# A decoder layer's cross-attention: weights turned by VectorE blocks and transfers through DRAM, exponentials per head, outputs one step later

## The chip, the cores and the metric

The kernel runs on one core of one Trainium2 chip. The core has engines that run side by side and wait for each other by semaphores: TensorE (PE in the profile, its weight loads PEld), VectorE (DVE), ScalarE (ACT), GpSimd (POOL) and SyncE (SP), whose queue here issues nearly all transfers to 16 DMA engines. SBUF is the working memory of 128 partitions, PSUM the one that TensorE writes to. The metric is device microseconds of one execution, lower is better; all data is float32.

## The reference

One post-norm decoder layer on x of 2 x 1024 x 256, with a context of 2 x 77 x 256, 16 heads of 64. Cut to what matters:

```python
x = _layernorm(x + self_attention(x))              # causal, rotary, Wq Wk Wv Wo, bo
# cross-attention, the part that is changed
q = (x @ w_q)  -> heads;  k, v = (ctx @ w_k), (ctx @ w_v) -> heads   # 77 keys
attn = softmax(q k^T / 8)                          # per head, over the 77 keys
x = _layernorm(x + concat_heads(attn @ v) @ w_o)
# feed-forward for half of the rows of each batch
weights = x @ w_r + b_r
selected = weights > (the 512th largest of 1024)
x = _layernorm(x + where(selected, gelu(x @ W1 + b1) @ W2 + b2, x))
```

## The kernel before

The self-attention runs first (to about 554 us of the profile) and is not touched. Then comes `Prepare`. It folds the cross-attention's weights: `fold_keys` multiplies w_q with the keys of the context into `wqk` (per batch 256 x (16 heads x 77 keys)), so that scores are one product of x1, the output of the first layernorm. `fold_values` multiplies the values with w_o into `vo` (16 x 77 rows of 256 columns per batch). `vo` goes through a DRAM tensor `vo_d` and comes back as `packed[b]`: the 1232 rows in ten chunks of 128 partitions (NK = 10, the last with 80 rows). So the output of a tile is ten products of turned weights with `packed[b]`.

A `Tile_` is 128 tokens; there are 16, eight for each batch. Its methods, with the lines of the profile:

- `scores(hh)` (L946 to L959), for half of the heads: TensorE writes 2 x 308 scores into one of two PSUM buffers `ps_x`; VectorE takes the maxima of eight heads (L953), then adds their negatives to the scores into `e` in SBUF (L955), which frees the PSUM buffer; ScalarE takes the exponentials of 616 columns in one instruction (L959).
- `weights(hh)`: VectorE sums each head (L964) and inverts (L966); GpSimd multiplies (L967).
- `transposes(ahead)`: TensorE turns `e`, ten blocks of 128 x 128 into PSUM (L978), ScalarE copies them into `p_t` (L984, L987). In the same PSUM tile the x1 of the tile three further on is turned (L983, L989).
- `output(midst, when)`: ten products po_cross (L998, two records each); VectorE adds x1 (L1000) and makes the layernorm (L114 to L121, with a power by GpSimd on L120). `close` writes the normalised rows and the router's weight of each row (`weigh`, L785).

The loop over s runs, on TensorE, the scores of tile s+1, the output of tile s-1, the transposes of tile s. In between stand the parts of the `Router` of batch 0 and later batch 1: `spread` (a transpose of the rows' weights and a copy by ScalarE), `reach` (VectorE counts, for the rows of a tile, how many weights they reach, L801), `select`, `slots`, `scatter` (GpSimd writes the rows to DRAM in order, L831), `load` (SP fetches them back). These are set at steps by the tables `ahead`, `at_end` and `midst`. After the loop come the last outputs and the feed-forward of batch 0, the last counts of batch 1, then batch 1's feed-forward.

The order of TensorE, VectorE and ScalarE is written out by hand: each runs its instructions in the order of the program text within the `with tc.manual_schedule(...)` at L1015. In the version before, SP's and GpSimd's order is left to the planner. The weights W1 and W2 of the feed-forward are loaded by two transfers of 1 MB (L95, L101), both issued at 572 us. Pools with `bufs=2` give two buffers to a tag, so the third use waits until the first is no longer read.

Of the kernel before, what the change touches and what calls it, by code (L numbers as in the profile page):

```python
# [20 lines left out]
S = 77  # L21
# [13 lines left out]
def decoder_layer(  # L35
# [55 lines left out]

    def load_wide(w, tag):

        t = wpool.tile([P, NC, INNER], F32, tag=tag, name=f"w_{tag}")
        nc.sync.dma_start(t, w.rearrange("(c p) n -> p c n", p=P))  # L95
        return t

    def load_tall(w):

        t = wpool.tile([P, NP, C], F32, tag="tall", name="w_tall")  # L100
        nc.sync.dma_start(t, w.rearrange("(c p) n -> p c n", p=P))  # L101
        return t
# [572 lines left out]
    class Prepare:  # L675
# [4 lines left out]
        def context(self, of):  # L680

            t = self.pool.tile([P, NP, B, S], F32, name=f"{of}T")
            for h2 in range(0, NP, 2):
# [11 lines left out]
                evacuate(t[:, h2 : h2 + 2, :, :], pk)  # L695
# [34 lines left out]
        def fold_values(self, v_t, b, first=0, last=NP, keep=evacuate):  # L730
# [17 lines left out]
            if last < NP:  # L748
                return
            full = HS // P  # L750
            nc.sync.dma_start(vo_d[b].rearrange("(h s) c -> s h c", s=S), vo)
            nc.sync.dma_start(packed[b][:, :full, :], vo_d[b, : full * P, :].rearrange("(k p) c -> p k c", p=P))
# [170 lines left out]

    class Tile_:


        def __init__(self, b, i):
            self.b, self.i = b, i
            self.x1 = x1s[b][:, i, :C]

        def turn(self):
            self.x_t = c2.tile([P, NC, P], F32, tag="x1T", name="x1T", bufs=3)
            pt = ring.tile([P, NC, P], F32, tag="t", name="pt_x")
            for c in range(NC):
                TE.transpose(pt[:, c, :], self.x1[:, c * P : (c + 1) * P], ident)
            A.copy(self.x_t, pt)

        def scores(self, hh):

            if hh == 0:  # L940
                self.e = c2.tile([P, H, S], F32, tag="e", name="e")
            ps = ps_x.tile([P, 2, NB], F32, tag="sx", name="ps_cross")
            for g in range(2):
# [7 lines left out]
            sc = ps[:, :, : Q * S].rearrange("p g (h s) -> p g h s", h=Q)  # L951
            top = small.tile([P, 2, Q], F32, tag="top2", name="top2")
            V.tensor_reduce(top, sc, AX.X, ALU.max, negate=True)  # L953
            e = self.e[:, hh * HH : (hh + 1) * HH, :]
            V.tensor_tensor(  # L955
                e.rearrange("p (g h) s -> p g h s", g=2), sc,
                top.unsqueeze(3).to_broadcast([P, 2, Q, S]), ALU.add,
            )
            A.activation(e, e, AF.Exp)  # L959

        def weights(self, hh):
            e = self.e[:, hh * HH : (hh + 1) * HH, :]
            sums = small.tile([P, HH], F32, tag="sums2", name="sums2")
            V.tensor_reduce(sums, e, AX.X, ALU.add)  # L964
            inv = small.tile([P, HH], F32, tag="inv2", name="inv2")
            V.reciprocal(inv, sums)  # L966
            G.tensor_tensor(e, e, inv.unsqueeze(2).to_broadcast([P, HH, S]), ALU.mult)  # L967

        def transposes(self, ahead=None):

            self.p_t = c2.tile([P, NK, P], F32, tag="pT2", name="pT2")
            e = self.e.rearrange("p h s -> p (h s)")
            for m in range(0, NK, 4):
                n = min(4, NK - m)
                pt = ring.tile([P, 4, P], F32, tag="t", name="pt_p2")
                for k in range(m, m + n):
                    w = min(P, HS - k * P)
                    self.turned = TE.transpose(pt[:w, k - m, :], e[:, k * P : k * P + w], ident).ins  # L978
                whole = n if (m + n) * P <= HS else n - 1
                if ahead and m + n == NK:  # L980
                    ahead.x_t = c2.tile([P, NC, P], F32, tag="x1T", name="x1T", bufs=3)
                    for c in range(NC):
                        TE.transpose(pt[:, n + c, :], ahead.x1[:, c * P : (c + 1) * P], ident)  # L983
                A.copy(self.p_t[:, m : m + whole, :], pt[:, :whole, :])  # L984
                if whole < n:
                    w = HS - (m + whole) * P
                    A.copy(self.p_t[:w, m + whole, :], pt[:w, whole, :])  # L987
                if ahead and m + n == NK:
                    A.copy(ahead.x_t, pt[:, n : n + NC, :])  # L989

        def output(self, midst=None, when=NK // 2):
# [8 lines left out]
            V.tensor_tensor(y, po, self.x1, ALU.add)  # L1000
            last = layernorm(self.x1, y)

            def close():
                last()
                routers[self.b].weigh(self.i)

            return close
# [7 lines left out]
    with tc.manual_schedule(engines={TE.engine, V.engine, A.engine}):  # L1015
# [3 lines left out]
        tiles[0].turn()  # L1019
        tiles[1].turn()  # L1020
        tiles[2].turn()
        first.fold_keys(k_t)
        v_t = first.context("v")
        first.fold_values(v_t, 0)
        first.fold_values(v_t, 1, 0, NP // 2)
        for hh in range(2):
            tiles[0].scores(hh)
        first.fold_values(v_t, 1, NP // 2, NP, A.copy)
        for hh in range(2):
            tiles[0].weights(hh)  # L1030
        for hh in range(2):
            tiles[1].scores(hh)
        for hh in range(2):
            tiles[1].weights(hh)
# [5 lines left out]
        w1 = load_wide(L0_ffn_W1, "wk")  # L1040
        w2 = load_tall(L0_ffn_W2)
# [19 lines left out]
        for s in range(B * NT - 1):  # L1061
# [13 lines left out]
            elif close:  # L1075
                close()
# [79 lines left out]
```

## Time and profile before

| | |
|---|---|
| time, median of 3 runs | 810.73 us (810.12 to 811.66) |
| profiled execution | 809.84 us |
| its span | 808.1 us |
| PE busy | 781.5 us (97%) |
| PEld, DVE, ACT, POOL busy | 77%, 72%, 44%, 45% |
| granted TensorE clock | 0.998 |
| preparation of the cross-attention | about 554 to 599 us |
| one step of the loop | 9.78 us |
| last output of the cross-attention ends | about 740.4 us |

The span is what the profile covers, from the first instruction to the last; the execution's time has 1.7 us more around it. A row of a timeline has its start, its length, the engine, the line, the operation and what it writes and reads, then how many instructions are merged in it; in brackets stands how long the engine was idle before it and whose work ended that. A row of DMA packets has the queue, the packets, their megabytes, and the time that they took as a share of 16 engines.

### The profile page before, as it was taken

The page shows a single profiled execution, that of the slowest core. Times are in us where ns is not written, and L with a number is a line of the kernel's source. Part 1 is how long each engine was busy: PE and PEld are TensorE (multiplying, and loading weights), DVE is VectorE, ACT ScalarE, POOL GpSimd, SP SyncE. Part 2 cuts the span into 40 slices and gives each one's busy share as a digit, 9 for nine tenths or more (in the row PEclk, how much of TensorE's full clock was granted, in tenths as well). Part 3 has the DMA queues.
Part 4 walks back from the last instruction along what each step waited for, and adds up shares of the span by engine and source line. Part 5 has one row for each costly group of instructions (what it writes and reads, how often), then busy time and mean ns, then how long its engine had stood idle before and what let it go on. Part 6 is the DMA issues. An engine that isn't in the chain of part 4 may idle for free.

```text
span 808.1 us, 26591 instructions
## 1 busy us (share of the span) xinstructions
PE 781.5 (97%) x11428; PEld 622.0 (77%) x11428; DVE 581.9 (72%) x1345; ACT 355.4 (44%) x842; POOL 367.7 (45%) x261
## 2 busy tenths in 40 slices
PE   8999999999999999999999988999999999999986
PEld 5565888888888888788788776688788888886745
DVE  2578678868778868678667796535577788888674
ACT  2565565655565556454554544102433332333130
POOL 2634455555375565365473553222033222261664
PEclk9999999999999999999999999999999999999999
DMA  5455477557567567668366467690450000011221
GB/s 195 129 148 177 129 210 209 171 168 211 157 169 230 158 179 223 174 171 204 112 198 185 133 185 158 173 324 3 168 187 1 1 1 0 1 53 53 68 91 52
DMA packets 65328, 112.32 MB, mean 139 GB/s; under 512 B 6497, under 2 KB 43707, under 8 KB 65211
## 3 DMA queue, kind: packets, MB, share of 16 engines
q1 hardware_dynamic: 59067, 89.64, 37.6%
q10 hardware_dynamic: 4608, 16.78, 7.5%
q0 software_dynamic: 1536, 4.20, 1.4%
q8 instruction: 90, 1.47, 0.8%
q14 instruction: 27, 0.22, 0.1%
HBM read 71.24 MB, written 22.59 MB: 116 GB/s over the span
## 4 chain that ended last, share of the span: by engine, by line
PE 82%; DVE 7%; POOL 4%; issue 4%; ACT 1%; DMA 1%; POOLq 0%; SPq 0%; ACTq 0%; DVEq 0%
PE po_self L410 17%; PE ps_scores L342 16%; PE pp_kq L268 13%; PE pp_v L303 7%; PE po_cross L998 6%; PE ps_cross L946 6%; PE po_proj L477 6%; PE pp_h L889 3%; PE po_ffn L900 2%; PE pt_p L978 1%; DVE pT L372 1%; DMA turned<-raw 1%; POOL comp L831 1%; POOL e L967 1%; DVE p L355 1%
## 5 line engine op out<-in xcount | busy, mean ns | idle before, releaser
L363 ACT ACTIVATE p<-p,neg 128x768 f32<-128x768 f32 (+7 forms) x256 | 196.3, 768 | 162.9 <-DVE neg L355 161.3
L355 DVE CUSTOM_DVE_ANT_0 p<-ps_scores,fence 128x512 f32<-128x512 f32 (+7 forms) x256 | 179.4, 750 | 104.9 <-PE ps_scores L342 104.5
L372 DVE STREAM_TRANSPOSE pT<-p 128x512 f32<-128x512 f32 (+7 forms) x256 | 175.7, 740 | 6.2 <-PE po_self L410 3.0
L410 PE MATMUL po_self<-pT,v 32*64 32x256 f32 (+6 forms) x7808 | 157.6, 295 | 10.1 <-issue 7.2
L410 PEld LDWEIGHTS po_self<-pT,v 32*64 32x64 f32 x7808 | 137.2, 130 | 34.9 <-issue 25.4
L342 PE MATMUL ps_scores<-kq 64*128 64x256 f32 (+3 forms) x1060 | 148.9, 411 | 1.8 <-DVE neg L355 1.0
L342 PEld LDWEIGHTS ps_scores<-kq 64*128 64x128 f32 x1060 | 93.3, 186 | 42.7 <-issue 28.2
L268 PE MATMUL pp_kq<-xT,w_pair 128*128 128x256 f32 (+2 forms) x524 | 118.6, 379 | 1.1 <-ACT xT L203 0.7
L291 POOL TENSOR_TENSOR turned<-turned,sin 128x1024 f32<-128x1024 f32 x31 | 73.2, 2362 | 93.0 <-DMA turned<-raw 80.1
L288 POOL TENSOR_TENSOR kq<-raw,cos 128x1024 f32<-128x1024 f32 x31 | 73.6, 2374 | 84.4 <-ACT raw L276 84.4
L268 PEld LDWEIGHTS pp_kq<-xT,w_pair 128*128 128x128 f32 x524 | 88.3, 190 | 23.9 <-issue 10.4
L967 POOL TENSOR_TENSOR e<-e,inv 128x616 f32<-128x616 f32 x32 | 38.2, 1215 | 113.0 <-DVE inv L966 67.2
L120 POOL TENSOR_TENSOR rs<-ve,neg_half 128x1 f32<-128x1 f32 x48 | 27.2, 570 | 107.2 <-DVE ve L118 105.2
L295 POOL TENSOR_TENSOR kq<-kq,turned 128x1024 f32<-128x1024 f32 x31 | 73.5, 2371 | 1.4
L998 PE MATMUL po_cross<-packed,pT 128*128 128x256 f32 (+1 forms) x320 | 72.5, 380 | 0.1
L946 PE MATMUL ps_cross<-wqk,x1T 128*128 128x308 f32 x256 | 69.2, 423 | 0.0
L998 PEld LDWEIGHTS po_cross<-packed,pT 128*128 128x128 f32 (+1 forms) x320 | 60.0, 190 | 9.4 <-ACT pT L984 0.3
L303 PEld LDWEIGHTS pp_v<-w_pair,xT 128*128 128x128 f32 x512 | 61.1, 192 | 4.0 <-issue 2.5
L303 PE MATMUL pp_v<-w_pair,xT 128*128 128x128 f32 x512 | 62.2, 275 | 0.0
L946 PEld LDWEIGHTS ps_cross<-wqk,x1T 128*128 128x128 f32 x256 | 47.4, 190 | 16.2 <-issue 0.7
L959 ACT ACTIVATE e<-e 128x616 f32<-128x616 f32 x32 | 23.0, 717 | 80.8 <-DVE e L955 80.8
L477 PE MATMUL po_proj<-wo,attnT 128*128 128x256 f32 x224 | 51.4, 381 | 0.3 <-ACT out_pair L424 0.3
(128 smaller groups left out, 817.0 us busy)
## 6 DMA issues: line engine op xcount, KB each, us to landing
turned<-raw SPq DMA_DIRECT2D x64, 256.0 KB, 4.7
v<-v_d ACTq DMA_DIRECT2D x32, 512.0 KB, 6.2
v<-v_d SPq DMA_DIRECT2D x32, 512.0 KB, 11.1
v_d<-v SPq DMA_DIRECT2D x16, 512.0 KB, 4.6
over<-inv_d SPq DMA_DIRECT2D x32, 256.0 KB, 4.8
attn_d<-out_pair SPq DMA_DIRECT2D x14, 512.0 KB, 4.3
attnT<-attn_d SPq DMA_DIRECT2D x8, 512.0 KB, 5.4
vo_d<-vo SPq DMA_DIRECT2D x2, 1232.0 KB
```

The source lines that it names most:

```text
L268: TE.matmul(pp[:, cols], self.w[:, c, "kq".index(of), :], x_ts[self.b, n][:, c, cols], start=(c == 0), stop=(c == NC - 1),)
L288: E.tensor_tensor(self.kq[:, :, n * NB : (n + 1) * NB], self.raw[n], self.twice(cos, n), ALU.mult)
L295: E.tensor_tensor(dst, dst, self.turned[n], ALU.add)
L303: TE.matmul(pv[:, i, :], x_ts[self.b, 2 * n // NT][:, c, toks], self.w[:, c, 2, :], start=(c == 0), stop=(c == NC - 1),)
L342: TE.matmul(self.ps[j][:, cols], self.kq[rows, 1, t * P : (t + 1) * P], self.kq[rows, 0, cols.start - at : cols.stop - at], start=True, st ...
L355: V.tensor_tensor_reduce(p[:, span], self.ps[j][:, span], fence[:, T - (t + 1) * P :], -SCALE, -MASKED, ALU.add, ALU.min, neg[:, i : i + 1],)
L363: A.activation(p[:, span], p[:, span], AF.Exp, bias=neg[:, i : i + 1], scale=-1.0, accum_out=self.sums[:, j, t : t + 1],)
L372: V.transpose(p_t[:, first : first + t * step + 1 : step, :], self.p[g, j][:, span].rearrange("p (n k) -> p n k", k=P),)
L410: ins = TE.matmul(self.po[r][j * D : (j + 1) * D, n:, :], self.v4[rows, NT * k + n, j * D : (j + 1) * D], p_t[rows, first:last:step, k * R ...
L477: TE.matmul(self.po, of, wo[:, c, :], start=(c == 0), stop=(c == NP - 1))
L946: TE.matmul(ps[:, g, : Q * S], self.x_t[:, c, :], wqk[:, c, self.b, h : h + Q, :].rearrange("p h s -> p (h s)"), start=(c == 0), stop=(c = ...
L998: TE.matmul(po, self.p_t[:w, k, :], packed[self.b][:w, k, :], start=(k == 0), stop=(k == NK - 1))
```

## The change

Five things are changed, all in the cross-attention.

1. The exponentials. VectorE only takes the maxima (`most`). ScalarE takes the exponentials of each head apart, straight from PSUM, with the negative maximum as bias and the sum of the head as second output (`exponentials`): 16 instructions for a tile. The addition and the sum on VectorE go away. The inversion and the multiplication become a function that is called later (`weights`).
2. The turning of weights for tiles 0 to 14. `blocks` lets VectorE turn 32 x 32 blocks of the whole `e` (1280 columns, the last 48 zero) into `part`, reading every fourth column, so that a row of `part` holds for each of four column classes 320 numbers. `part` goes to DRAM in one transfer; `fetch` brings it back in four, one for 32 tokens each, into the layout of `p_t`: runs of 32 numbers, 128 bytes. Tile 15 is still turned by TensorE.
3. The output of a tile comes two steps after its scores' step instead of one (`tiles[s - 2].output()` beside `tiles[s + 1].scores`). `e` gets two fixed buffers, `e_all`.
4. SP's order is now part of the order written by hand. The two halves of `packed[0]` follow the first fetch; those of `packed[1]` stand at the ends of steps 3 and 4; W1 and W2 are loaded in four transfers of 512 KB at the ends of steps 5 to 8.
5. The preparation is ordered anew: scores of tiles 0 to 3 stand between the products of `Prepare`, and their copies are mostly given to VectorE (`keep=V.tensor_copy`). The x1 transposes of tiles 3 and 4 are there too; later ones follow the output in each step. The router's parts move by a step or within a step.

```diff
+        def pack(self, b, h):
             full = HS // P
-            nc.sync.dma_start(vo_d[b].rearrange("(h s) c -> s h c", s=S), vo)
-            nc.sync.dma_start(packed[b][:, :full, :], vo_d[b, : full * P, :].rearrange("(k p) c -> p k c", p=P))
+            a, e = (0, full // 2) if h == 0 else (full // 2, full)
+            nc.sync.dma_start(packed[b][:, a:e, :], vo_d[b, a * P : e * P, :].rearrange("(k p) c -> p k c", p=P))
+            if h == 0:
+                return
             nc.sync.dma_start(packed[b][: HS - full * P, full, :], vo_d[b, full * P :, :])
...
+    e_all = c1.tile([P, 2, NK * P], F32, name="e_all")
+    G.memset(e_all[:, :, HS:], 0.0)
...
-            sc = ps[:, :, : Q * S].rearrange("p g (h s) -> p g h s", h=Q)
-            top = small.tile([P, 2, Q], F32, tag="top2", name="top2")
-            V.tensor_reduce(top, sc, AX.X, ALU.max, negate=True)
-            e = self.e[:, hh * HH : (hh + 1) * HH, :]
-            V.tensor_tensor(
-                e.rearrange("p (g h) s -> p g h s", g=2), sc,
-                top.unsqueeze(3).to_broadcast([P, 2, Q, S]), ALU.add,
-            )
-            A.activation(e, e, AF.Exp)
-
-        def weights(self, hh):
-            e = self.e[:, hh * HH : (hh + 1) * HH, :]
-            sums = small.tile([P, HH], F32, tag="sums2", name="sums2")
-            V.tensor_reduce(sums, e, AX.X, ALU.add)
-            inv = small.tile([P, HH], F32, tag="inv2", name="inv2")
-            V.reciprocal(inv, sums)
-            G.tensor_tensor(e, e, inv.unsqueeze(2).to_broadcast([P, HH, S]), ALU.mult)
+        def most(self, hh):
+            self.top = small.tile([P, 2, Q], F32, tag="top2", name="top2")
+            V.tensor_reduce(self.top, self.split(hh), AX.X, ALU.max, negate=True)
+
+        def exponentials(self, hh):
+
+            sums = self.sums = small.tile([P, HH], F32, tag="sums2", name="sums2")
+            sc, top = self.split(hh), self.top
+            for h in range(HH):
+                g, q = divmod(h, Q)
+                A.activation(
+                    self.e[:, hh * HH + h, :], sc[:, g, q, :], AF.Exp, bias=top[:, g, q : q + 1],
+                    accum_out=sums[:, h : h + 1],
+                )
+            inv = small.tile([P, HH], F32, tag="inv2", name="inv2")
+
+            def weights():
+                V.reciprocal(inv, sums)
+                e = self.e[:, hh * HH : (hh + 1) * HH, :]
+                self.ready = G.tensor_tensor(e, e, inv.unsqueeze(2).to_broadcast([P, HH, S]), ALU.mult).ins
+
+            return weights
+
+        def blocks(self):
+
+            part = c2.tile([P, 4, NK * R32], F32, tag="part", name="part")
+            V.transpose(
+                part.rearrange("p c (k q) -> p c k q", q=R32), self.whole.rearrange("p (k q c) -> p c k q", q=R32, c=4)
+            )
+            part_d = dram.tile([P, 4, NK * R32], F32, tag="part", name="part_d")
+            nc.sync.dma_start(part_d, part)
+            self.p_t = c2.tile([P, NK, P], F32, tag="pT2", name="pT2")
+
+            def fetch():
+                for g in range(4):
+                    rows = slice(g * R32, (g + 1) * R32)
+                    nc.sync.dma_start(
+                        self.p_t[:, :, rows], part_d[rows, :, :].rearrange("j c (k q) -> (j c) k q", q=R32)
+                    )
+
+            return fetch
...
-    with tc.manual_schedule(engines={TE.engine, V.engine, A.engine}):
+    with tc.manual_schedule(engines={TE.engine, V.engine, A.engine, nc.sync.engine}):
...
+        tiles[0].scores(0)
+        tiles[0].scores(1)
+        held = most(tiles[0])
+        v_t = first.context("v", V.tensor_copy)
+        for f in held:
+            f()
+        first.fold_values(v_t, 0, 0, NP // 2)
+        fetch = tiles[0].blocks()
+        first.fold_values(v_t, 0, NP // 2, NP)
+        fetch()
+        first.pack(0, 0)
+        first.pack(0, 1)
+        tiles[1].scores(0)
+        tiles[1].scores(1)
+        held = most(tiles[1])
+        first.fold_values(v_t, 1, 0, NP // 2, V.tensor_copy)
+        for f in held:
+            f()
+        tiles[2].scores(0)
+        kept = [t.turn() for t in tiles[3:5]]
+        tiles[2].scores(1)
+        tiles[2].most(0)
+        tiles[1].blocks()()
+        for keep in kept:
+            keep(V.tensor_copy)
+        held = [tiles[2].exponentials(0)]
+        tiles[2].most(1)
+        held.append(tiles[2].exponentials(1))
+        first.fold_values(v_t, 1, NP // 2, NP - 2, V.tensor_copy)
+        tiles[3].scores(0)
+        first.fold_values(v_t, 1, NP - 2, NP, V.tensor_copy)
+        tiles[3].scores(1)
+        for f in held:
+            f()
...
-        for s in range(B * NT - 1):
-            if s > 0:
-                for hh in range(2):
-                    tiles[s + 1].scores(hh)
...
-            close = tiles[s - 1].output(midst.get(s), NK - 2) if s > 0 else None
-            tiles[s].transposes(tiles[s + 3] if s + 3 < B * NT else None)
...
+        bulk = {
+            5: lambda: nc.sync.dma_start(w1[:, 0, :], wide1[:, 0, :]), 6: lambda: nc.sync.dma_start(w1[:, 1, :], wide1[:, 1, :]),
+            7: lambda: nc.sync.dma_start(w2[:, :m, :], tall2[:, :m, :]), 8: lambda: nc.sync.dma_start(w2[:, m:, :], tall2[:, m:, :]),
+        }
+        for s in range(2, B * NT - 1):
+            t = tiles[s + 1]
+            for hh in range(2 if s > 2 else 0):
+                t.scores(hh)
+            t.most(0)
+            held = [t.exponentials(0)]
+            ahead.get(s, none)()
+            tiles[s].blocks()()
+            t.most(1)
+            held.append(t.exponentials(1))
+            counts.get(s, none)()
+            held[0]()
+            norm = tiles[s - 2].output()
+            if s + 3 < B * NT:
+                tiles[s + 3].turn()()
+            close = norm()
+            held[1]()
+            close()
+            at_end.get(s, none)()
+            if s in (3, 4):
+                first.pack(1, s - 3)
+            elif s in bulk:
+                bulk[s]()
+        close = tiles[-3].output()()
         tiles[-1].transposes()
+        close()
+        norm = tiles[-2].output(lambda: (r1.spread(4, 6), reaches(r1, range(4), 4, 6)), 4)
```

## The prediction

> **What bounds the kernel now.** I read the chain of waits first, cut to the cross-attention stage, then busy times in the same steps, then the DMA packets. The chain, in order of time (start, length, what):
>
> ```profile
> 609.00 4.15 PE ps_cross L946 x16
> 613.15 4.32 PE po_cross L998 x20
> 617.47 1.09 PE pt_p L978 x10
> 618.56 0.22 PE pt_p L983 x2
> 618.78 4.15 PE ps_cross L946 x16
> ```
>
> One step of the loop is 9.78 us, and TensorE fills all of it: scores 4.15, outputs 4.32, ten transposes of weights 1.09, two of x1 0.22. Nothing else ever ends last. The busy times of that step (length, PE, PEld, DVE, ACT, POOL, clock, DMA share, GB/s) show what is left over elsewhere:
>
> ```profile
> 608.84:618.62 9.78, 9.78 (x51) 8.10 (x50) 7.06 (x15) 3.09 (x8) 2.93 (x3) 1.00 0.01 2
> ```
>
> VectorE has 2.7 us free, ScalarE 6.7, and the DMA engines do nothing at all. So a microsecond off TensorE is a microsecond off the time here, until something else takes 8.7 us per step.
>
> **TensorE's part.** The ten transposes leave TensorE for tiles 0 to 14; tile 15 keeps them. 15 x 1.09 = 16.4 us gained, the whole of the gain. Scores, outputs and x1 transposes stay, so the new step is 4.15 + 4.32 + 0.22 = 8.69 us.
>
> **ScalarE.** Two exponentials of 616 (0.72 each) and five copies of transposes (1.24 + 0.28) become 16 exponentials of 77 with a bias and a sum. The nearest rows are the self-attention's, which have both:
>
> ```profile
> 322.51 0.39 ACT L363 ACTIVATE p<-p,neg 128x128 f32<-128x128 f32 x1
> 322.80 0.19 ACT L363 ACTIVATION_READ_ACCUMULATOR p<-p,neg 128x1 f32 x1
> 322.90 0.70 ACT L363 ACTIVATE p<-p,neg 128x512 f32<-128x512 f32 x1
> ```
>
> From one start to the next after it, 128 elements take 0.39 us, reading the sum included. The same line takes 493 ns at 256 elements and 388 at 128, 0.82 ns an element, so 77 elements take 0.39 - 0.04 = 0.35. Per step 16 x 0.35 + one copy of x1 0.39 = 6.0 us. If nothing overlapped it would be 0.35 + 0.19 = 0.54 each and 9.0 us, above 8.69. I take 6.0, since the row shows the overlap directly.
>
> **VectorE.** Gone: two additions (0.80 each) and two sums (0.76 each), 3.1 us. Added: one block transpose of 1280 columns. Its row in the self-attention takes 1199 ns for 1024 and 1059 for 896, so 1280 take 1199 + 256 x 1.09 = 1.48; its input now steps over four elements, which no row shows: 1.48 if that costs nothing, 3.0 if it halves the rate. I take 1.5, as the row. VectorE falls from 7.06 to about 5.5 us per step; the counts of the router add 2 to 3.2 in six steps, 8.7 at worst, level with TensorE.
>
> The score buffers (two in PSUM) are freed later, after eight exponentials instead of one addition. Following one step from its start: scores(0) done at 2.1, maximum until 3.1, exponentials until 5.9; the block transpose holds the second maximum until 5.4, its exponentials end at 8.7. The buffers are wanted at 8.7 and 10.8. Covered, by 2 us.
>
> **The DMA path, the new resource.** Each tile now sends 640 KB to DRAM (rows of 5 KB) and fetches 640 KB in four transfers of runs of 128 bytes: 5120 packets, 320 for each of 16 DMA engines. SP's queue is in program order, so a fetch waits for its store to land, and the next store stands behind that fetch. No row shows packets of 128 bytes. Three windows bound them (packets in 0.5 us at 4 bytes, the load of b1; in 1 us at 1 KB; in 0.8 us at 512 bytes):
>
> ```profile
> q1 hardware_dynamic: 712, 0.02, 88.7%
> ...
> q1 hardware_dynamic: 377, 0.39, 109.3%
> ...
> q1 hardware_dynamic: 521, 0.27, 112.7%
> ```
>
> Engine time over packets: 0.5 x 16 x 0.887 / 712 = 10.0 ns at 4 bytes; 46 ns at 1 KB; 28 ns at 512 bytes. The three lie on one line, so 128 bytes take about 14 ns, with 10 and 28 as the ends. A fetch is 320 x 14 = 4.5 us (3.2 to 9.0). A store at the 426 GB/s of the window 574.5 to 576.0 is 1.5 us. Between a store's last bytes and the first of the load that waits for it stands this (start, length on SP):
>
> ```profile
> 597.31 0.39 SPq L752 DMA_DIRECT2D packed<-vo_d  x1
> ```
>
> The store's last packets end near 596.9 and this load's first come near 598.3, 1.4 us. The fastest landing of a 512 KB store is 3.3 us against 1.3 for its bytes; I take 1.8. So one tile occupies the path for 1.5 + 1.8 + 4.5 = 7.8 us, less than 8.69, with 0.9 to spare. Hiding the latency: blocks end 5 us into a step and the outputs of that tile start 4.2 us into the step after next, 16.6 us later; the path needs 1.1 + 7.8 + 0.5 = 9.4. That is what the step of delay covers.
>
> The spare is used up where other transfers share the queue: two halves of packed_1 (1.6 us each, steps 3 and 4) and four loads of 512 KB for W1 and W2 (1.3 us, steps 5 to 8), which before ran at 572 to 603 beside nothing. There the path takes 9.1 to 9.4 us, 0.4 to 0.7 above TensorE's step, and the stall falls on po_cross.
>
> **Start and end.** Before, preparation kept TensorE full (44.1 of the 45 us from 554 to 599). Now scores wait for exponentials: following the order by hand with the prices above, scores of tile 2 and 3 wait 0.1, 0.6, 0.8 and 0.8 us for their buffers, since VectorE also empties all of vo_1 (eight copies of 0.69): 2.3 us. The fetch for tile 2 comes behind the store of vo (1.2 MB, 4.5 us at 267 GB/s): 0.2. Steps 5 to 9 then wait 0.7, 0.4, 0.5, 0.5, 0.5 = 2.6. At the end tile 14 is needed only 14 us after its step began, while scattered rows share the engines: 1.0. From the last output on (740.4) nothing differs.
>
> Sum: -16.4 + 2.3 + 0.2 + 2.6 + 1.0 = -10.3 us. The profiled execution took 809.84 (span 808.1 and 1.7 around it): 799.5. The median is 0.9 above it: 800.4.
>
> [...] The row shows 4-byte packets of 10 ns and no step below 512 bytes. [...]
>
> **Rivals.**
> Packets (slower). Beyond 8.69 us the path sets the step, 13 times. The gain left after start and end is 13 us; 6 us of other transfers come on top, so it turns to a loss where 13 x (cycle - 8.69) + 6 > 13: a cycle of 9.2, a fetch of 5.9, a packet of 18.5 ns. At the 512-byte row's pitch (0.8 x 16 / 521 = 24.6 ns): fetch 7.9, cycle 11.2, 13 x 2.5 + 6 - 13 = +26 us, 836. For: no such packet in the trace, and a wide window of strided 512-byte reads shows 56 ns (336 packets in 1 us at 118.5%). Against: the 10 ns row.
> Fully hidden (faster still). At 10 ns the cycle is 6.5 and with other transfers 8.1: only start and end cost, -16.4 + 3.3, so 797.6. For: the 4-byte row. Against: 512 bytes cost 28.
> An engine's chain binds. If the stepped transpose takes 3.0 us, the second exponentials end 1.5 later and VectorE needs up to 10.2 in the six counting steps: about 1 us each, 806.5. If exponentials don't overlap, 0.3 x 13: 804. For: neither form is in the trace. Against: its nearest rows.
> No change, 810: packets near 18 ns.
>
> **How the numbers follow.** Forecast 0.42, fully hidden 0.13, engine chain 0.11, packets 0.30, no change 0.04. Predicted 800.4; its own range is 797 to 805. Eight times in ten: 795, below fully hidden, to 826, which leaves out half of the packet rival (0.15). About 0.2% is what a measurement tells from no change: faster 0.64, same 0.04, slower 0.32.
>
> **What would show it.** Right: steps of 8.7 us from the tenth tile on with po_cross back to back; fetches of 4.5 us; 0.35 us between exponentials; a transpose of 1.5. Wrong: po_cross idle behind the fetched tile in every step (packets), ps_cross idle behind an exponential (chain), or SP's issue of a fetch taking more than the 0.64 us that b1's load took.

## The result, and the profile after

The changed kernel takes 818.51 us (median of 4 runs, 816.33 to 819.46) beside 810.67 for the kernel before (4 runs): a ratio of 1.0092, 95% interval 1.0069 to 1.0114. It is 0.9% slower, where 1.3% faster was forecast. The span of the profiled execution is 816.5 us, 8.4 above that of before.

TensorE lost its transposes, as meant. Its busy time fell from 781.5 to 773.9 us, and yet its share of the chain that ended last fell from 82% to 72%, with DMA's up from 1% to 6%. These are the page's totals and the chain's shares by engine:

```profile
PE 773.9 (95%) x11278; PEld 609.7 (75%) x11278; DVE 581.7 (71%) x1306; ACT 388.8 (48%) x1251; POOL 368.0 (45%) x262
...
PE 72%; DVE 9%; DMA 6%; POOL 5%; issue 4%; ACT 2%; SPq 1%; POOLq 0%; DVEq 0%; ACTq 0%
```

So TensorE does less and waits more. The busy times of four stretches from one output to the next (columns as in the forecast's table: stretch, length, PE, PEld, DVE, ACT, POOL, clock, DMA share, GB/s) show three kinds of step:

```profile
703.87:712.64 8.77, 8.77 (x40) 7.10 (x40) 7.95 (x18) 5.38 (x33) 3.38 (x4) 1.00 0.66 149
662.76:673.20 10.44, 9.64 (x42) 7.21 (x40) 9.64 (x23) 5.64 (x34) 2.90 (x3) 1.00 0.82 179
641.41:652.31 10.90, 8.85 (x41) 6.83 (x39) 10.04 (x19) 6.90 (x41) 2.90 (x3) 1.00 0.79 173
652.31:663.43 11.12, 10.86 (x41) 8.42 (x41) 6.81 (x15) 4.67 (x28) 2.94 (x3) 0.85 0.70 165
```

The first is the step that was forecast, with TensorE full for 8.77 us. In the second VectorE is busy for 9.64 of 10.44. The third ends with a wait for a fetch. The fourth has the whole of TensorE's time taken, but at a clock of 0.85.

TensorE's own instructions in order of time (start, length; in brackets the idle time ahead and who ended it) show the third and fourth:

```profile
645.95 4.31 PE L943 MATMUL ps_cross<-wqk,x1T 128*128 128x308 f32 x16
652.31 6.27 PE L1011 MATMUL po_cross<-packed,pT 128*128 128x256 f32 x20 [2.05 <-DMA pT<-part_d]
```

Before, 20 records of po_cross took 4.48 us. Here they wait 2.05 for p_t, and then take 6.27.

What the fetch was late for is seen in SP's queue. First a stretch with a load of W1, then one without:

```profile
645.88 3.42 SPq L988 DMA_DIRECT2D pT<-part_d  x4
649.34 0.79 SPq L1114 DMA_DIRECT2D w<-in_L_ffn_W_dram  x1
650.22 0.38 SPq L982 DMA_DIRECT2D part_d<-part  x1
657.22 3.80 SPq L988 DMA_DIRECT2D pT<-part_d  x4
...
688.86 3.55 SPq L988 DMA_DIRECT2D pT<-part_d  x4
692.52 0.85 SPq L982 DMA_DIRECT2D part_d<-part  x1
696.29 3.49 SPq L988 DMA_DIRECT2D pT<-part_d  x4
```

From fetch to fetch the path takes 7.43 us without other loads (7.8 was forecast), and 11.34 with one (9.1 to 9.4 was). From store to fetch it is 3.77 against 7.00: the load in front of the store costs 3.2 us, not its own 1.3. This is the largest case: behind the other three loads of W1 and W2 store to fetch is 5.7 to 6.0 us and the cycle 10.5 to 10.6, and the two further cycles without a load are 7.8 and 7.4. VectorE isn't in this: the blocks that the store at 650.22 takes, tile 6's, were done at 643.76.

From 658 to 700 us, where the path needs 10.5 us for each tile, VectorE does too, and there the chain that ended last does not touch TensorE at all. One turn of it (start, length, what), from one maximum (`top`) to the next; `part` is the block transpose, `reach` the router's counting, `e_all` GpSimd's multiply, `rs` its power for the layernorm, `x` the layernorm's last instruction:

```profile
662.40 0.71 DVE top L954
663.11 2.40 DVE part L978
665.52 0.68 DVE top L954
666.20 2.77 DVE reach L794 x10
...
669.26 1.15 POOL e_all L971
670.43 0.56 POOL rs L108
671.01 1.31 DVE x L109
...
672.84 0.71 DVE top L954
```

A turn is 10.44 us. Two pieces are longer than the rows that the forecast went by: the block transpose at 2.4 to 2.5 us, and the layernorm's last instruction, 1.31 us, where L121 took 0.41 before for the same 256 columns:

```profile
609.68 0.41 DVE L121 TENSOR_SCALAR x<-y,mv,rs 128x256 f32<-128x256 f32 x1 [0.66 <-POOL rs L120]
```

One piece of the forecast is seen as it was meant. ScalarE's exponentials follow each other at 0.31 us, the read of the sum included:

```profile
663.21 0.33 ACT L962 ACTIVATE e_all<-ps_cross,top 128x77 f32<-128x77 f32 x1 [4.00 <-DVE top L954]
663.43 0.19 ACT L962 ACTIVATION_READ_ACCUMULATOR e_all<-ps_cross,top 128x1 f32 x1
663.52 0.32 ACT L962 ACTIVATE e_all<-ps_cross,top 128x77 f32<-128x77 f32 x1
```

And so is the price of a packet: 4 us in which little but a fetch ran (697 to 701) hold

```profile
q1 hardware_dynamic: 4230, 0.54, 85.0%
```

that is 4 x 16 x 0.85 / 4230 = 12.9 ns for each packet (14 was forecast).

**A measure for what follows.** The same program up to the changed stage reaches the product for the keys (pp_k) between 548.5 and 560.5 us in the fourteen traces of this case, and what follows the last po_cross takes 67.4 to 70.1. So beside the ratio to the kernel before, which ran on the same chip each time, I give the *stage*: from the start of pp_k to the end of the last po_cross in the profiled execution. It is 186.1 us before and 190.8 after; the forecast meant 175.8. Each stage is of one execution. Four kernels (the changed one and those of experiments 3, 9 and 11) are the same up to the fetch of tile 2. Its output waits 2.44, 3.72, 4.14 and 1.83 us for that fetch in their traces, and then takes 4.56 to 6.89, so two stages with the path through DRAM can differ by 4.6 us without a reason in the change.

### The profile page after: what moved, and what is told of

Its sections match the earlier page's. It is cut to its first block, busy times and chain, and to the rows that moved or that the text cites. A ratio compares the mean times of both kernels' runs of the same rounds, so it can differ in the third digit from the quotient of the medians.

```text
span 816.5 us, 26772 instructions
## 1 busy us (share of the span) xinstructions
PE 773.9 (95%) x11278; PEld 609.7 (75%) x11278; DVE 581.7 (71%) x1306; ACT 388.8 (48%) x1251; POOL 368.0 (45%) x262
## 4 chain that ended last, share of the span: by engine, by line
PE 72%; DVE 9%; DMA 6%; POOL 5%; issue 4%; ACT 2%; SPq 1%; POOLq 0%; DVEq 0%; ACTq 0%
PE po_self L398 17%; PE ps_scores L330 16%; PE pp_kq L256 12%; PE pp_v L291 6%; PE po_proj L465 6%; PE po_cross L1011 4%; PE pp_h L882 3%; PE ps_cross L943 2%; DMA turned<-raw 2%; DVE part L978 2%; DVE reach L794 2%; PE po_ffn L893 2%; DMA part_d<-part 2%; DMA pT<-part_d 2%; POOL e_all L971 1%
## 5 line engine op out<-in xcount | busy, mean ns | idle before, releaser
L962 ACT ACTIVATE e_all<-ps_cross,top 128x77 f32<-128x77 f32 x256 | 79.0, 337 | 61.0 <-DVE top L954 59.8
L256 PEld LDWEIGHTS pp_kq<-xT,w_pair 128*128 128x128 f32 x524 | 88.9, 192 | 23.8 <-issue 10.6
L1011 PE MATMUL po_cross<-packed,pT 128*128 128x256 f32 (+1 forms) x320 | 76.1, 394 | 12.0 <-DMA pT<-part_d 9.9
L971 POOL TENSOR_TENSOR e_all<-e_all,inv 128x616 f32<-128x616 f32 x32 | 38.9, 1220 | 105.4 <-DVE inv L969 105.0
L1011 PEld LDWEIGHTS po_cross<-packed,pT 128*128 128x128 f32 (+1 forms) x320 | 62.1, 197 | 23.5 <-issue 8.0
L962 ACT ACTIVATION_READ_ACCUMULATOR e_all<-ps_cross,top 128x1 f32 x256 | 56.1, 219 | 0.0
```

Of the source, the lines that this page charges most:

```text
L256: TE.matmul(pp[:, cols], self.w[:, c, "kq".index(of), :], x_ts[self.b, n][:, c, cols], start=(c == 0), stop=(c == NC - 1),)
L962: A.activation(self.e[:, hh * HH + h, :], sc[:, g, q, :], AF.Exp, bias=top[:, g, q : q + 1], accum_out=sums[:, h : h + 1],)
L1011: TE.matmul(po, self.p_t[:w, k, :], packed[self.b][:w, k, :], start=(k == 0), stop=(k == NK - 1))
```

## The experiments

T1 is the theory that the transfer path sets the loss, T2 that VectorE's chain does. All diffs are against the changed kernel.

**1. Longer runs.**

```diff
-    self.p_t[:, :, rows], part_d[rows, :, :].rearrange("j c (k q) -> (j c) k q", q=R32)
+    self.p_t.rearrange("p k n -> p (k n)")[:, g * NK * R32 : (g + 1) * NK * R32],
+    part_d[rows, :, :].rearrange("j c n -> (j c) n")
```

> The fetch brings the same bytes in runs of 1280 B (512 packets a tile) instead of 128 B (5120); they land in another order within a row of p_t, so the weights of a block of four tiles of tokens are mixed up and the output differs. Theory T1 (the transfer path of one queue, its small packets above all, sets the loss): landing of a fetch falls from 6.1 us after its first issue to under 4, the path cycle without extras from 7.6 to under 6, both waits of 2.44 and 2.05 us for pT go, and with them the two po_cross of 6.2 us; time 803 to 808. Theory T2 (VectorE's chain in the counting steps sets it): the steps around 663 to 694 us keep 10.4 us, only the first waits go; time 811 to 814.

Measured: 801.40 us, ratio 0.9878 (0.9799 to 0.9958); stage 179.0. No po_cross waits for pT, and a tile's twenty take 4.48 to 4.57 us throughout. A fetch is issued in 1.74 us instead of 3.42. But pt_r, the transpose of `spread`, still waits 1.09 and 1.53 us for `route`, the rows' weights by VectorE. T1 holds for the larger part: 11.8 us of the stage hang on the fetch.

**2. The block transpose's stride.**

```diff
-    part.rearrange("p c (k q) -> p c k q", q=R32), self.whole.rearrange("p (k q c) -> p c k q", q=R32, c=4)
+    part.rearrange("p c n -> p (c n)"), self.whole
```

> The block transpose reads e in plain order (stride 1) instead of every fourth column; size and output the same, so the rows of p_t no longer belong to the rows of packed and the output differs. T2: the transpose takes 1.5 us instead of 2.48, VectorE is busy 8.7 instead of 9.7 us in steps 7 to 9, their period falls to 9.5, time 813 to 816. T1: the transpose gets shorter, but the fetch issues in steps 5 to 8 stay 10.5 us apart; 817.5 to 819. If the stride is not the reason, the transpose stays at 2.48 us.

Measured: 813.55 us, ratio 1.0068 (1.0030 to 1.0105); stage 189.8. The group of the transpose (busy, mean ns, idle before) in the changed kernel and in this one:

```profile
L978 DVE STREAM_TRANSPOSE part<-e_all 128x1280 f32<-128x1280 f32 x15 | 37.2, 2483 | 3.2 <-POOL e_all L971 3.2
```
```profile
L978 DVE STREAM_TRANSPOSE part<-e_all 128x1280 f32<-128x1280 f32 x15 | 22.5, 1502 | 3.6 <-POOL e_all L971 3.6
```

The stride costs 0.98 us for each tile, 15 us of VectorE's time in all. Taking it away moves the stage by 1.0, which is less than one wait differs between traces; the interval of the ratio overlaps that of the changed kernel, and 1.0068 of 810.67 us, 816.2, lies between the two expectations. The fetches bind: po_cross waits 2.96, 3.94, 1.17, 0.57, 1.07 and 2.31 us for them. Why every fourth column takes 2483 ns and plain order 1502 is not shown; no run tried another stride.

**3. Loads on another queue.**

```diff
-    5: lambda: nc.sync.dma_start(w1[:, 0, :], wide1[:, 0, :]),
+    5: lambda: nc.scalar.dma_start(w1[:, 0, :], wide1[:, 0, :]),
...
```

> The four loads of W1 and W2 in steps 5 to 8 are issued on ScalarE's queue instead of SP's; nothing else moves. T1 in its form 'one queue': store to fetch in those steps falls from 5.7 to 7.0 us towards 3.8, the fetch issues come 8.7 to 9 us apart instead of 10.5, time 811 to 814. T1 in its form 'shared DMA engines': the bytes still share the engines, store to fetch stays above 5 us, time 816 to 818. T2: steps 7 to 9 keep 10.4 us, since VectorE is busy 9.7 of them, at most 1.5 us come back; 817 to 818.5.

Measured: 813.36 us, ratio 1.0025 (0.9984 to 1.0066), so about 0.7% better than the changed kernel. Its profile is of one of its longer executions (817.5 us), with a stage of 193.6 us, so the two readings don't agree. From 662 to 730 us no output waits for a fetch, but steps of 10.1 and 10.6 us remain, now with pt_r waiting 1.04 and 1.44 us for `route`. Store to fetch is 3.3 to 4.8 us behind those four steps, as the form 'one queue' has it. Before that stand waits of 3.72 us (tile 2, behind the store of vo), 1.39 and 3.51 (behind the halves of packed_1, still on SP's queue), and at the end one of 3.25. It is inconclusive on how much time the four loads cost; it does show VectorE's chain next in line.

**4. No transfers at all.**

```diff
-    part_d = dram.tile([P, 4, NK * R32], F32, tag="part", name="part_d")
-    nc.sync.dma_start(part_d, part)
-    self.p_t = c2.tile([P, NK, P], F32, tag="pT2", name="pT2")
...
+    self.p_t = packed[self.b][:, :, :P]
+    return lambda: None
```

> The store of the blocks and the four fetches of each tile are left out, the block transpose stays; the outputs of tiles 0 to 14 use a part of packed in place of the weights, so the output differs. T1: no wait for pT, no po_cross over 4.6 us, W loads no longer matter; all steps but those held by spread at 8.7 us; time 798 to 803. T2: the first waits go, but steps 7 to 9 keep 10.0 to 10.5 us; time 806 to 811.

Measured: 798.52 us, ratio 0.9858 (0.9790 to 0.9926); stage 179.0, the same as with long runs. It fits neither theory alone. The time is T1's, but from 651.8 us on the steps take 10.1, 10.6, 8.7 and 11.0: in the first two pt_r waits 1.09 and 1.54 us for `route`, in the last the scores wait 0.64 and 0.75 for exponentials, and T1 allowed more than 8.7 only where `spread` holds a step. By the ratios the changed kernel lies 19 us above this one (13 to 25 by the two intervals), more than the 11.8 of the stages; where the rest lies stays open.

**5. Straight into p_t.** The blocks lie in SBUF, and p_t does too; the way through DRAM isn't needed.

```diff
-    part_d = dram.tile([P, 4, NK * R32], F32, tag="part", name="part_d")
-    nc.sync.dma_start(part_d, part)
...
-    self.p_t[:, :, rows], part_d[rows, :, :].rearrange("j c (k q) -> (j c) k q", q=R32)
+    self.p_t[:, :, rows], part[rows, :, :].rearrange("j c (k q) -> j c k q", q=R32)
```

> The store of the blocks to DRAM is left out: four transfers a tile go from the blocks in SBUF straight into p_t, with the same 5120 runs of 128 B; the output is the reference's. Theory T1 (the transfer path sets the loss) in the form 'store, wait and fetch in a row': the transfers start where the blocks end instead of 2.3 to 3.7 us later, nothing is queued behind a wait for a store, all waits for pT over 0.5 us go; from the start of pp_k to the last po_cross 179 to 182 us (before 186.1, after 190.8, without transfers 179.0), time 0.986 to 0.992 of before. T1 in the form 'the small packets': 5120 packets keep their 6.1 us to landing, waits for pT remain in the steps with loads of W1 and W2; 184 to 188 us, 0.995 to 1.003 of before.

Measured: 807.28 us beside 812.97, ratio 0.9921 (0.9893 to 0.9949); stage 179.8. One wait for pT is left, 1.64 us at the last fetched tile. So 5120 packets of 128 bytes for each tile do fit, if no store and no wait between stands in their row: the first form of T1. Here they come from SBUF and not from DRAM, so the small packets of the old fetch aren't tried alone; with long runs (experiment 1) the store and the wait stayed and were hidden as well. What is left binds in VectorE, seen in three steps of this run (columns as above):

```profile
651.50:661.60 10.10, 9.03 (x41) 6.98 (x39) 9.30 (x23) 5.65 (x34) 2.90 (x3) 1.00 0.62 129
661.60:672.20 10.60, 9.17 (x40) 7.07 (x40) 9.80 (x27) 5.55 (x34) 2.91 (x3) 1.00 0.60 116
681.00:691.80 10.80, 9.54 (x43) 7.27 (x41) 9.88 (x19) 5.39 (x33) 4.03 (x4) 1.00 0.49 81
```

VectorE is busy for all of them but 0.8 to 0.9 us, the most of which is L109's wait for GpSimd's power (0.66).

**6. L109 first.** On top of the direct transfer:

```diff
-                def close():
+                def close(between=lambda: None):
                     last()
+                    between()
                     routers[self.b].weigh(self.i)
...
-            close = norm()
-            held[1]()
-            close()
+            norm()(held[1])
```

> As the direct transfer, and in each step the last instruction of the layernorm (L109) is put ahead of the second reciprocal and GpSimd's second multiply instead of behind them. Theory T2 (the rest of the loss is VectorE's chain, in which L109 is held by GpSimd's multiply): L109 falls from a mean of 1.04 or 1.30 us to 0.41 in the steps, the waits of pt_r for route (1.09 and 1.53 us without transfers) fall by 0.9 each or more, 1 to 3 us less than the direct transfer alone. If L109 is not held by GpSimd: it keeps its length, and the second multiply, now later, delays the next blocks; 0 to 2 us more.

Measured: 808.12 us, ratio 0.9914 (0.9875 to 0.9953); stage 179.7, no less. L109's mean over its 32 instances with x fell from 740 to 528 ns, and pt_r's waits from 1.07 and 1.43 to none and 0.87. All of it was given back: GpSimd's second multiply now comes later, and the idle time of the block transpose behind it grew from 3.2 to 7.8 us over the fifteen. L109 does hang on GpSimd's multiply, and moving it alone brings nothing.

**7. TensorE turns again.** Part of the change undone: `tiles[s].transposes()` stands where `blocks` and the fetch stood.

> TensorE transposes all tiles as in the kernel before (ten transposes a tile, ScalarE copies them), the block transpose and its transfers are gone; the exponentials by ScalarE, the outputs one step later and the loads in pieces stay. T1 and T2 alike: no wait for pT, the step is 9.78 us again. If the other two parts of the change cost and gain nothing but the 2.3 us at the start and 1 at the end: 0.999 to 1.006 of before. If they carry part of the loss (ScalarE's sixteen exponentials with three copies more, the order of VectorE): 1.008 or more. If the later outputs bring something by themselves: under 0.998.

Measured: 855.15 us, ratio 1.0500 (1.0450 to 1.0549). That is over the 1.008 of the second outcome, but far over, and for a reason that none of the three names. The steps take 11.7 us. ScalarE's copies into p_t wait 3.8 us in the mean (48.8 over 13 waits) for po_cross of two tiles before, whose buffer they fill: transposes two steps ahead of the output need three buffers, and ScalarE's exponentials, and TensorE behind them, stand behind the copy. So it said nothing on the other parts, and was run again with the third buffer.

```diff
-    self.p_t = c2.tile([P, NK, P], F32, tag="pT2", name="pT2")
+    self.p_t = c2.tile([P, NK, P], F32, tag="pT2", name="pT2", bufs=3)
```

> TensorE transposes all tiles, as in the earlier run of this form, but with three buffers of p_t, so that ScalarE's copies no longer wait for the output of two tiles before. If that wait was the reason for its step of 11.7 us: the step falls to 9.8 to 10.2 us, stage 190 to 198 us, time 1.005 to 1.02 of before. If it was ScalarE's order (copies between two groups of exponentials, which TensorE's scores wait for): the step stays above 11 us, 1.03 to 1.05.

Measured: 824.83 us, ratio 1.0220 (1.0175 to 1.0265); stage 203.3, over the 198 expected. Where nothing is counted, outputs come 9.79, 9.78 and 9.78 us apart: the step of before, to 0.01 us. So exponentials by ScalarE and outputs one step later neither cost nor gain there, and the step's gain is all in the transposes. In the counting steps `spread`'s copy now waits behind ScalarE's copies and exponentials, 1.8 to 2.1 us each time; that cost belongs to this form alone, and how the two other parts do at the ends stays open.

**8. The stride again, with the transfers hidden.** Direct transfer and plain order of e together.

> As the direct transfer, and the block transpose reads e in plain order (so the rows of p_t no longer belong to the rows of packed; the output differs). T2 (with the transfers hidden, VectorE's chain is the limit in the counting steps, 9.3 to 9.9 us busy of 10.1 to 10.8): each of these steps gives back about 1.0 us, the stage from pp_k to the last po_cross falls from 179.8 to 175 to 177 us. If the remaining wait is not VectorE's work but the chain through GpSimd's multiplies and ScalarE: 179 to 180 as with L109 put first.

Measured: 799.56 us, ratio 0.9878 (0.9834 to 0.9923); stage 177.8, 2.0 less than the direct transfer alone. That is less than T2's 2.8 to 4.8. Its parts are larger: up to the output at 630.38 us it is 1.9 shorter, from there to the one at 704.21 another 2.8, and the second wait of pt_r falls from 1.43 to 0.43. The end gives 2.7 back, since the last fetch is waited for 2.18 us (1.64 there), and the eight and twelve records of po_cross behind it take 3.04 and 3.20 us (1.97 and 2.76 there).

**9. Loads behind the store.** The same bytes on the same queue, in another order:

```diff
     nc.sync.dma_start(part_d, part)
+    behind()
...
-    if s in (3, 4):
-        first.pack(1, s - 3)
-    elif s in bulk:
-        bulk[s]()
+    more = (lambda: first.pack(1, s - 4)) if s in (4, 5) else bulk.get(s - 1, none)
+    tiles[s].blocks(more)()
```

> The changed kernel with its halves of packed_1 and of W1 and W2 issued right behind the store of the blocks (steps 4 to 9) instead of ahead of it; every byte stays on SP's queue. T1 (the path is a sum on one queue: what stands ahead of a store delays it, and the fetch behind it, by the whole of its transfer): the extra runs in the store's own latency of 2 us and more; store to fetch falls from 5.7 to 7.0 us to 4 to 5, stage from 190.8 to 184 to 188 us, time 1.000 to 1.006 of before. If the bytes alone count (the engines are full): the fetch now waits behind the extra instead, same sum, 189 to 192 us.

Measured: 809.64 us, ratio 1.0015 (0.9990 to 1.0041); stage 189.9. The ratio is as T1 had it, the stage is not. In SP's queue the order did what was meant:

```profile
651.16 0.33 SPq L982 DMA_DIRECT2D part_d<-part  x1
651.53 0.43 SPq L1115 DMA_DIRECT2D w<-in_L_ffn_W_dram  x1
654.60 3.56 SPq L989 DMA_DIRECT2D pT<-part_d  x4
```

Store to fetch is 3.4 us with 512 KB between them, where the load in front made it 7.00. In the other three steps with loads of W1 and W2 it is 3.5 to 3.8, and 2.9 to 3.1 in the next four without. So most of what the load cost was its place, and about 0.5 us its bytes. From 630 to 720 us no output waits for a fetch; the counting steps still take 10.1 and 10.6 us, through pt_r's waits of 1.07 and 1.43. The rest of this profile's stage is at the start, where the fetch of tile 2 came 4.14 us late behind the store of vo and the po_cross behind it took 6.89 us. In the changed kernel these were 2.44 and 6.24; the difference of 2.35 us is not the order's, so the order gained more than the stage shows.

**10. VectorE's order, with the transfers hidden.** On top of the direct transfer, the last counting instruction of steps 6 to 10 moves between GpSimd's second multiply and L109, so that both waits of the chain are filled with work. In step 9 the moved one also counts 128 columns that had an instruction of their own, some 0.3 us less work:

```diff
+    after_held = {
+        6: lambda: r0.reach(2, 0, 4), 7: lambda: r0.reach(3, 0, 4), 8: lambda: r0.reach(4, 0, 6),
+        9: lambda: r0.reach(5, 0, 7), 10: lambda: r0.reach(6, 0, NT),
+    }
...
     held[1]()
+    after_held.get(s, none)()
     close()
```

> As the direct transfer, and in steps 6 to 10 the last counting instruction (0.74 to 1.27 us) stands between GpSimd's second multiply and L109; the output is the reference's. T2 with the lock between GpSimd and VectorE: the multiply runs beside the counting, L109 falls from 1.3 to 0.41 us there and its wait of 0.66 us for rs goes; 1.3 to 1.5 us less in each of steps 6 to 10, so stage 179.8 to 174 to 177 us, time 0.982 to 0.988 of before. If counting is held by the multiply as L109 was: it gets longer by about the same 0.9 us, 178 to 180 us.

Measured: 798.29 us beside 808.21, ratio 0.9873 (0.9834 to 0.9912); stage 176.1, 3.7 less than the direct transfer alone (the intervals of the two ratios overlap a little, and the traces show where the 3.7 come from). VectorE in one of these steps (start, length):

```profile
665.75 0.19 DVE L969 RECIPROCAL inv<-sums 128x8 f32<-128x8 f32 x1
665.87 1.09 DVE L794 TENSOR_SCALAR_CACHE_REDUCE reach<-every,route 128x896 f32<-128x896 f32 x1
666.88 0.08 DVE L794 DVE_READ_ACCUMULATOR reach<-every,route 128x1 f32 x1
666.88 1.02 DVE L109 TENSOR_SCALAR x<-y,mv,rs 128x256 f32<-128x256 f32 x1
```

and GpSimd beside it:

```profile
666.54 1.22 POOL L971 TENSOR_TENSOR e_all<-e_all,inv 128x616 f32<-128x616 f32 x1
```

The wait for `rs` is gone. GpSimd's multiply runs from 666.54 to 667.76; counting beside it takes 1.09 us for 896 columns (1.14 in the kernel before), and L109, which begins inside it, ends at 667.90, again just behind its end: 1.02 us, where 0.41 was expected. The lock of the expectation is a name for no more than this: L109 ends just behind the multiply that it begins in, and counting beside the multiply keeps its length. What makes the two differ is not shown. This version is faster than both kernels.

**11. Both orders, through DRAM.** The loads behind the store and the late counting, with store and fetches as they are in the changed kernel:

> The changed kernel with its store to DRAM and fetches as they are, and both orders mended: the halves of packed_1 and of W1 and W2 go right behind the store of the blocks, and the last counting instruction of steps 6 to 10 stands between GpSimd's second multiply and L109. The output is the reference's. Theory of two limits of about the same height (the path and VectorE's chain, each of which takes over when only the other is relieved: 189.8 us for the stage with the one, 189.8 with a shorter block transpose): together they bring 4 to 7 us more than the loads behind the store alone, stage 183 to 186 us, time 0.992 to 0.998 of before; what stays are the waits for pT at the start (tile 2, 2 to 4 us) and at the end (2 to 4 us), and po_cross at half clock behind them. If the path alone is the limit and the store must go to gain anything: 188 to 190 us, 1.000 to 1.006 of before.

Measured: 807.01 us beside 809.46, ratio 0.9961 (0.9933 to 0.9990); stage 180.3, below the 183 expected. One order alone left the stage at 189.9 (loads), and a VectorE lighter by 1 us in each step at 189.7; both orders give 9.5 us more than the loads alone. That part includes the start, where tile 2 waited 1.83 us here and 4.14 there, with 2.3 us more in its output behind it: 4.6 of the 9.5, which the edit has no part in. The steps from 639.5 to 712.6 us hold 3.6, and the end 1.2.

## Why the prediction was wrong

The mechanism of the gain was right: steps with nothing else in them are 8.7 to 8.8 us (703.87 to 712.64), and the step with TensorE's transposes is 9.78. The stage came out 15.0 us above the forecast, 190.8 for 175.8, and the runs split that in two.

**The transfers, 11.8 us where 3.8 were forecast.** With no transfers the stage is 179.0. The terms were 0.2 for tile 2, 2.6 for steps 5 to 9 and 1.0 for the end.

- The path by itself was right: 7.4 us for 7.8, packets of 12.9 ns for 14, SP's issue under it. The rival of the packets (from 18.5 ns) did not happen.
- The step that failed is "There the path takes 9.1 to 9.4 us". I added each load's own 1.3 to 1.6 us to the sum, as if a load in front cost what it takes. Between store and fetch it cost 1.9 to 3.2 us, SP's issue of it 0.8 to 0.9 more, and the cycle was 10.5 to 11.3. The five outputs from 652 to 699 us waited 2.05, 0.26, 0.65, 1.56 and 0.45 us for their fetches, 5.0 for the 2.6 forecast. Put behind the store, a load adds about 0.5 us between store and fetch. What makes 1.9 to 3.2 of 1.3 I can't say from these runs: the load's bytes meet the fetch still running (its issue ends at 649.30, its data is there at 652.3), and then the store's bytes meet the load's.
- The start was 0.2 by the forecast and 2.44 us in the profile, since the fetch of tile 2 could be issued only 8.9 us after its store at 606.95, which stood behind that of vo. The end was 1.0 for tile 14; tile 13 waited 2.53, and tile 14 another 2.04, which the profile puts down to `route`.
- "the stall falls on po_cross" was right, but each stall was counted once. Two of them, 2.44 and 2.05 us, were followed by a po_cross at a lower clock (0.73 in the mean): 1.8 us more each. No term had that.
- Two numbers on the way were off and changed little. The window of the 10.0 ns also held 19 packets of 1 KB; without them, at 46 ns each, it is 9.0. And the 6 us of other transfers in the rival of the packets are 8.4 by their own prices, two of 1.6 and four of 1.3.

**VectorE, most of 7.0 us where nothing was forecast.** Without transfers the stage is still 7.0 above the 172.0 that the other terms give, and its three long steps (10.1, 10.6 and 11.0 for 8.7) hold 5.6 of that. "8.7 at worst, level with TensorE" failed twice. The transpose took 2.48 us, between the two ends that were set (1.48 and 3.0), and I took the lower; and L109 went from 0.41 to 1.3, by an overlap with GpSimd that the new order creates. 8.7 with 1.0 and 0.9 on top is 10.6, beside turns of 10.4 to 10.8 in the profile. The rival "an engine's chain binds" named the right place. Its size, up to 10.2 us, came close partly by luck: it knew one of the two causes, and priced that at 3.0. The late counting gives back 3.7 of the 7.0. The other 3.3 are not settled; small waits of scores for exponentials (0.5 to 0.75 us around step 11) are among them.

**Where the rivals stood.** They were priced as alternatives, and here two held at once, the path at 10.5 to 11.3 us and VectorE at 10.4 to 10.8. That is why a lighter VectorE alone (experiment 2) changed next to nothing, why hiding the path (experiments 1, 4 and 5) gave 11 to 12 us and then left steps of 10.1 to 11.0, and why no single wait in the profile has the size of the loss. The start's waits of scores came out at 2.3 us as a sum, but that is partly luck: they are 0.16, 1.20, 0.27 and 0.65 for 0.1, 0.6, 0.8 and 0.8, the largest is put down to VectorE's copy of x1, and the last belongs to tile 4.

Of the 8.4 us between the two spans, 4.7 are in the stage, 1.4 ahead of it and 2.4 behind it. The last two lie within what the same code varies by in these traces, and I don't ascribe them to the change.

## What to carry to other kernels

In an ordered queue, a transfer is priced by what stands behind it (store to fetch took 7.00 us with 512 KB ahead of the store, 3.4 with them behind it, 3.77 without a load): a bulk load belongs behind the issue whose latency it can use, not ahead of one that the next step waits for. When work moves off the bounding engine, sum every other resource with its waits included: two of them near the new limit hide each other (here 10.5 to 11.3 and 10.4 to 10.8 us, for 8.7), and an experiment that relieves one shows only how far it stood above the other. And before data goes through DRAM to change partitions, try the transfer inside SBUF: it drops a store, a wait and half of the bytes, here 11.0 us of the stage (190.8 to 179.8).

## What the runs showed of the hardware that was not expected

- A block transpose of 128 x 1280 float32 takes 1502 ns in plain order and 2483 when it reads every fourth column.
- A tensor_scalar of 256 columns takes 0.41 us alone and mostly 1.3, up to 1.4, beside GpSimd's multiply of 616, ending just behind it; counting with a sum isn't held (1.09 us beside it, 1.14 before).
- SP issues a transfer of 1280 packets in 0.85 us (3.42 for four), and one of 128 packets and the same bytes in 0.43 (1.74 for four).
- TensorE's clock after a wait. In the changed kernel's trace, stretches at half clock begin a whole number of 3.41 us apart (621.96 and 652.68 us: nine). Counted in windows of such a grid, waits of 2.05 and 2.53 us in the changed kernel and, last, one of 3.72 in experiment 3 (stretch, length, PE, clock, DMA share, GB/s):

```profile
649.27:652.68 3.41, 1.36 (x6) 1.00 1.07 140
652.68:656.09 3.41, 3.41 (x10) 0.50 0.74 304
724.36:727.78 3.42, 1.82 (x9) 1.00 1.03 263
727.78:731.19 3.41, 2.48 (x12) 1.00 0.39 148
```
```profile
614.33:617.74 3.41, 1.56 (x7) 1.00 0.82 130
617.74:621.16 3.42, 1.56 (x7) 1.00 0.87 256
```

The wait of 2.05 us lies whole in one window, and the next runs at 0.50. The longer ones are cut by a border into 1.60 and 0.94, and into 1.85 and 1.86, and the clock stays at 1.00. So what parts these three is not the length of the wait but how much of it falls into one window. Over the stages of the fourteen traces, 760 windows, the clock was at half after all 13 with TensorE idle for 1.89 us or more, and after none with 1.86 or less; in the changed kernel's it was after 2.44 and 2.05, and after none with 1.80 or less. Ahead of the stage idle time doesn't part them so: in the changed kernel there is a fall after 0.83 us (at 468.36 us), and none after 1.12 (at 482.02). What sets the grid and the fall is not shown.
